# Attention's last head: layer-norm parts at every pair of source blocks, and the widest unit of targets second in a head

## The chip, the cores and the metric

The kernel runs on one core of a Trainium2 chip. The metric is the device time of one execution in microseconds (us). Five engines work side by side and are tied by semaphores: PE (TensorE, matmuls), ACT (ScalarE), DVE (VectorE), POOL (GpSimd) and SP (SyncE, which here issues the DMAs). An instruction waits in its engine's order until what it needs is done.

## The reference

A graph of 6250 nodes with 128 features and 206,250 directed edges (100,000 drawn both ways, and a loop at each node) goes through four graph layers. Each is followed by a residual and a layer norm:

```python
x = _layernorm(x + _L0_gnn_ref(...))   # mean of the neighbours, two products
x = _layernorm(x + _L1_gnn_ref(...))   # a two-layer product for every edge, mean over the edges of a target
x = _layernorm(x + _L2_gnn_ref(...))   # sums over the neighbours, two products
x = _layernorm(x + _L3_gnn_ref(...))   # attention, four heads of 32 features
```

The change lies in the last one, attention:

```python
h = (x @ W).reshape(N, H, C)                       # H = 4 heads, C = 32
logits = a_src[src] + a_dst[dst]
logits = jnp.where(logits > 0, logits, 0.2 * logits)
e = jnp.exp(logits - seg_max[dst])
alpha = e / (segment_sum(e, dst)[dst] + 1e-16)
out = segment_sum(h[src] * alpha[:, :, None], dst)
out = out.reshape(N, H * C) + bias
out = (out - mean) * rsqrt(var + 1e-05) * gamma + beta
return relu(out)
```

So a node's row passes two layer norms at the end: the one inside attention, then relu, the residual, and the outer one, whose result is the output.

## The kernel before, in words

The first three layers take the time up to about 3950 us and are not touched. Attention (`attend`, line 1107) works without gathers. The graph stands in HBM as a dense matrix of edge counts, `adj`, in bf16, cut into blocks of 128 source nodes by 256 targets. 6250 nodes make 49 source blocks. The targets make 12 groups of 512 and a last group of 106 (line 99). Two groups form a unit (line 1120), and the last, small group is joined to the sixth unit as its `more` (line 1122): five units of 1024 targets and a wide one of 1130. A pass of one unit in one head is called a step here: 4 heads x 6 units = 24 steps, in the order of `steps` (line 1247).

A step runs over the 49 source blocks in 25 pairs (line 1283; the last pair has one block). For each pair:
- SP loads the pair's block of `adj` into `A` three pairs ahead (`load`, line 1250; four buffers), and for the wide unit a narrow block into `Am`.
- ACT makes `r`, one instruction for each of the two blocks (line 1293), from the target's and the source's terms. It has two buffers.
- DVE takes the minimum `B` of `A` and `r` (line 1300) and the difference `C` of `A` and `B` (line 1302): the edges whose logits are on one side of zero, and the rest. In a wide step two more instructions do the same for the 106 targets (`Bm`, lines 1306 and 1307).
- PE multiplies the head's tables with `B`, `A` and `C` and adds up in PSUM over the step (line 1320, ten matmuls of 512 columns a pair; line 1322 for the 106 targets).

Everything else is let in between the pairs by hand, by three lanes (`Lane`, line 1226). A lane holds generators. `step(now)`, called once after each pair, runs the first generator up to its next `yield`, if `now` has reached `due`. Then `due` is set to now plus what was yielded, or plus 2 where nothing was; a generator that ends sets it to `now`, so that the next begins at the next pair. The lanes are:
- `sums`: `targets` (line 1180) prepares the target terms of the next step (transposes on PE, copies by ACT, lines 1186 and 1194). `close` (line 1197) finishes the step before: ACT and DVE copy the sums out of PSUM (lines 1202, 1205), PE folds them (line 1212), and four small DVE instructions divide (lines 1216 to 1221), for each group. In the last head it then hands `finish3` of the group to `ends` (line 1224).
- `news`: `tables` (line 1158) makes the next head's tables, group after group, four parts each: two DVE instructions (lines 1164, 1166), then three casts by ACT (line 1169), with a subtraction on POOL (line 1171) after the first two, and a DVE instruction with the next group's first part (line 1174). It is added at a head's second step (line 1282); what is left of it when the next head begins is run then (line 1280).
- `ends`: `finish3` (line 617) with `layernorm` (line 351) and `update` (line 369). Its parts, one for each `yield`: add and statistics (DVE); square root (ACT, line 361); reciprocal and scaling (DVE, lines 363, 365); gain and offset (DVE, lines 622, 623); relu (ACT, line 625); residual and statistics (DVE); square root (ACT); reciprocal and scaling (DVE); and then the store, issued by SP (line 126).

After the last step the lanes are emptied, one after the other (last line of `attend`): `close` of the last unit, then all of `ends`.

Of the kernel before, what the change touches and what calls it, by code (L numbers as in the profile page):

```python
# [68 lines left out]
def kernel(  # L69
# [688 lines left out]
    def fast():  # L758
# [348 lines left out]
        def attend(acc, al):  # L1107
# [12 lines left out]
            units = [(g[0][0], g, []) for g in (groups[k : k + 2] for k in range(0, len(groups), 2))]  # L1120
            if len(units) > 1 and len(units[-1][1]) == 1 and units[-1][1][0][2] == 1:
                units[-2][2].extend(units.pop()[1])
            with tc.tile_pool(name="f3c", bufs=1) as one, tc.tile_pool(name="f3", bufs=2) as ep, \
                    tc.tile_pool(name="f3n", bufs=1) as pool, \
                    tc.tile_pool(name="f3s", bufs=6, space=PSUM) as sps, \
# [100 lines left out]
                class Lane:  # L1226


                    def __init__(self):
                        self.left, self.due = [], 0  # L1230

                    def add(self, fn):
                        self.left.append(fn)
# [1 line left out]
                    def step(self, now):  # L1235
                        if self.left and now >= self.due:
                            lag = next(self.left[0], self)
                            if lag is self:
                                self.left.pop(0)
                            self.due = now if lag is self else now + (lag or 2)  # L1240

                    def rest(self):
                        while self.left:
# [16 lines left out]
                            nc.sync.dma_start(more_of[i][:, :n].rearrange("p l q -> p (l q)"),  # L1260
                                              adj[more[0][0] // (2 * P), :, a * 2 * P : (a + n) * 2 * P])

                sums, news, ends = Lane(), Lane(), Lane()
                for i in range(3):
                    load(i)
                drain(targets(0, *steps[0]))
# [1 line left out]
                made, i, now = 0, 0, 0  # L1268
# [69 lines left out]
        with tc.tile_pool(name="facc", bufs=1) as one:  # L1338
            acc = one.tile([P, 3, NA], F32, name="acc")
            for k in range(3):  # L1340
                nc.vector.memset(acc[:, k, :], 0.0)

            two, third = [acc[:, k, 0 : NB * D].bitcast(BF16).rearrange("p (b k d) -> p k b d", k=2, d=D) for k in (1, 2)]
            parts = [two[:, 0], two[:, 1], third[:, 0]]
            mlp("f1", lambda *a: node1(acc, parts, *a))
            al = one.tile([P, 2, NB, HEADS], F32, name="al")
            nc.vector.memset(al, 0.0)
            dense2(parts, lambda *a: node2(acc, al, *a))
            attend(acc, al)
# [39 lines left out]
```

## Time and profile before

| | us |
|---|---|
| median of 3 runs | 5586.52 (5569.49 to 5587.32) |
| profiled execution, its own time | 5547.28 |
| its span, first to last instruction | 5545.3 |
| first to last B of attention (line 1300) | 3958.39 to 5478.63 |
| PE busy over the span | 4983.3 (90%) |
| DVE busy | 3011.7 (54%) |
| ACT busy | 2590.3 (47%) |
| POOL busy | 1927.6 (35%) |
| mean granted TensorE clock | 0.94 |

The shares are means over stages with different limits, so they say little about attention alone. The steps of the last head, from the first B of each to the next step's first B, take 59.38, 62.69, 64.92, 64.47, 62.45 and, for the wide step, 74.12 to its last B; 66.67 are left from there to the span's end. In the third head they take 59.21, 60.70, 60.12, 60.22, 60.03 and 67.34. A row of a timeline has the start in us from the span's start, the length in us, engine, line, operation, out<-in with shapes, the count, and in brackets the idle time before it and what ended it.

### The profile page before, as it was taken

How to read it: one execution, taken by the hardware profiler on the slowest of the kernel's cores; microseconds unless marked ns; L12 is line 12 of the kernel's file. 1: busy time of each engine (PE TensorE's matmuls, PEld its weight loads, DVE VectorE, ACT ScalarE, POOL GpSimd, SP SyncE). 2: the span in 40 equal slices, each digit the busy share in tenths (PEclk: the TensorE clock that was granted, in tenths of full speed). 3: DMA queues.
4: the chain of work that ended last, by engine and by line, in shares of the span. 5: the costliest groups of instructions: out<-in, count | busy, mean ns of one | idle time of the engine just before them, and what ended most of it. 6: DMA issues, size and time to landing. Idle time of an engine off the chain costs nothing. (4 is left out here: it accounts for less than half of the span.)

```text
span 5545.3 us, 90483 instructions
## 1 busy us (share of the span) xinstructions
PE 4983.3 (90%) x33855; PEld 4094.6 (74%) x33855; DVE 3011.7 (54%) x5036; ACT 2590.3 (47%) x3581; POOL 1927.6 (35%) x1919
## 2 busy tenths in 40 slices
PE   1999997899999999998999999899799999999995
PEld 0899997888888888888888888699555655555553
DVE  4787874233333333333333333222488888888998
ACT  2444442332323333333322333100499999998884
POOL 2232223665666666666666665000111010010000
PEclk9999998898989988889988999899899999999997
DMA  3433323444444444444444443455367777777773
GB/s 75 130 143 120 142 114 128 128 129 123 128 123 129 129 127 127 124 124 129 130 123 127 126 125 102 163 187 187 120 200 218 224 213 227 217 210 227 212 211 119
DMA packets 587578, 837.61 MB, mean 151 GB/s; under 512 B 117853, under 2 KB 482330, under 8 KB 576384
## 3 DMA queue, kind: packets, MB, share of 16 engines
q1 hardware_dynamic: 502537, 605.23, 35.4%
q0 software_dynamic: 83472, 224.21, 14.0%
q8 instruction: 271, 4.44, 0.3%
q10 hardware_dynamic: 1124, 2.31, 0.1%
q14 instruction: 174, 1.43, 0.1%
HBM read 739.88 MB, written 91.53 MB: 150 GB/s over the span
## 5 line engine op out<-in xcount | busy, mean ns | idle before, releaser
L129 POOL DMA_INDIRECT g<-t,src_i x1617 | 1578.1, 976 | 965.0 <-issue 735.9
L1293 ACT ACTIVATE r<-ad,bias 128x1024 bf16<-128x1024 f32 (+1 forms) x1176 | 1276.7, 1155 | 91.1 <-DVE B L1300 55.4
L1068 DVE TENSOR_TENSOR g<-g,pre 128x512 f32<-128x512 f32 x882 | 549.5, 641 | 1340.5 <-PE pre L1066 406.8
L1320 PEld LDWEIGHTS <-acc 128*99 128x99 bf16 x5856 | 698.2, 126 | 606.5 <-issue 157.2
L1080 PE MATMUL seg<-oh,g 128*128 128x64 f32 (+1 forms) x6468 | 1026.1, 282 | 36.6 <-issue 34.5
L1066 PE MATMUL pre<-W1s,eaT 128*128 128x256 f32 (+1 forms) x3234 | 900.9, 420 | 117.9 <-DVE g L1068 68.2
L1080 PEld LDWEIGHTS seg<-oh,g 128*128 128x128 f32 (+1 forms) x6468 | 950.8, 203 | 75.0 <-issue 43.2
L1320 PE MATMUL s<-B,acc 128*99 128x512 bf16 x3504 | 885.1, 382 | 89.3 <-DVE B L1300 83.4
L1069 ACT ACTIVATE g<-g 128x512 f32<-128x512 f32 x882 | 506.7, 592 | 714.9 <-DVE g L1068 506.4
L1066 PEld LDWEIGHTS pre<-W1s,eaT 128*128 128x128 f32 (+1 forms) x3234 | 638.3, 210 | 250.5 <-issue 121.2
L1300 DVE TENSOR_TENSOR B<-A,r 128x2048 bf16<-128x2048 bf16 x600 | 724.5, 1207 | 118.8 <-ACT r L1293 91.4
L1057 ACT COPY eaT<-tp 128x512 f32<-128x512 f32 (+1 forms) x441 | 241.2, 547 | 1038.8 <-PE tp L1055 341.1
L1080 PE MATMUL seg<-oh,ea 128*128 128x64 f32 (+1 forms) x3234 | 659.6, 286 | 25.2 <-issue 24.9
L1080 PEld LDWEIGHTS seg<-oh,ea 128*128 128x128 f32 (+1 forms) x3234 | 523.0, 203 | 24.6 <-issue 24.3
L930 ACT CAST A<-pa 128x784 bf16<-128x784 f32 x400 | 322.8, 813 | 328.2 <-PE pa L927 319.6
L800 PE MATMUL sum<-A,xs 128*128 128x256 bf16 (+1 forms) x3675 | 467.1, 273 | 0.0
L1302 DVE TENSOR_TENSOR C<-A,B 128x1024 bf16<-128x1024 bf16 x600 | 429.6, 716 | 64.9 <-PE s L1320 2.4
L1171 POOL TENSOR_TENSOR xs<-xs,acc 128x264 f32<-128x264 f32 (+1 forms) x104 | 103.2, 999 | 985.4 <-ACT acc L1169 985.4
L800 PE MATMUL sum<-A,acc 128*128 128x256 bf16 (+1 forms) x3675 | 407.6, 271 | 8.6 <-DMA A<-adj 8.6
L927 PE MATMUL pa<-oh,oh 128*128 128x98 bf16 x3200 | 356.2, 269 | 59.6 <-ACT A L930 56.1
L800 PEld LDWEIGHTS <-acc 128*128 128x128 bf16 x3675 | 355.0, 98 | 49.2 <-issue 8.9
L800 PEld LDWEIGHTS <-xs 128*128 128x128 bf16 x3675 | 357.4, 101 | 34.6
(230 smaller groups left out, 4422.2 us busy)
## 6 DMA issues: line engine op xcount, KB each, us to landing
A<-adj SPq DMA_DIRECT2D x2304, 128.0 KB
ea<-in_edge_attr_dram SPq DMA_DIRECT2D x292, 256.0 KB
A<-adj SPq DMA_DIRECT2D x25, 1600.0 KB
A<-adj SPq DMA_DIRECT2D x25, 1536.0 KB
ea<-in_edge_attr_dram SPq DMA_DIRECT2D x146, 192.0 KB
g<-t,src_i POOLq DMA_INDIRECT x1617
Am<-adj SPq DMA_DIRECT2D x96, 128.0 KB
t<-y SPq DMA_DIRECT2D x24, 256.0 KB
```

What stands on the lines that cost most here:

```text
L129: nc.gpsimd.indirect_dma_start(out=to, out_offset=None, in_=table, in_offset=bass.IndirectOffsetOnAxis(ap=index[:K, t : t + 1], axis=0))
L800: nc.tensor.matmul(ps[:, :n], parts[part][:, b, :], a(b)[:, :n], start=k == 0, stop=k == 3 * NB - 1)
L927: nc.tensor.matmul(ps[:, o, q * LO : (q + 1) * LO], ohs[g][0][:, 2 * j + o, :, q], ohs[g][1][:, 2 * j + o, :, q], start=True, stop=True)
L930: nc.scalar.copy(A[sb][:, :, q0 : q0 + 2 * QI].rearrange("p k (o q) -> p k o q", q=QI), ps[:, :, : QI * LO].rearrange("p o (q k) -> p k o ...
L1066: nc.tensor.matmul(pre[:K, t, :], eaT[i][:, b + t, :K], W1s[:, 1, :], start=True, stop=True)
L1068: nc.vector.tensor_add(gb, gb, pre[:K, :n, :])
L1069: nc.scalar.activation(gb, gb, AF.Relu)
L1080: nc.tensor.matmul(ps[:, m, :], rows, oh[c][:K, a + t, :], start=a + t == 0 and m == 0, stop=a + t == T - 1, skip_group_check=True)
L1293: nc.scalar.activation(r[:, l, : n + m], ad[:, : n + m], AF.Relu, bias=bias[:, b + l, h : h + 1], scale=BIG)
L1300: nc.vector.tensor_tensor(wide(bt), At[:, :ns, :kk, :w], wide(r), ALU.min)
L1302: nc.vector.tensor_sub(ct[:, :n].rearrange("p (s q) -> p s q", q=w), At[:, :ns, 0, :w], bt[:, 0, :n].rearrange("p (s q) -> p s q", q=w))
L1320: nc.tensor.matmul(s[to][g][:M, : c1 - c0], row, rhs(c0, c1), start=to not in begun, stop=stop)
```

## The change

Two edits in `attend`. The wide unit, when the small group has been joined to it, is taken out of the last place of the list of units and put at the second. The list is used by all four heads. And a lane gets its lag as an argument: `ends` is made with 1, so that a part of `finish3` follows after one pair and not two; `sums` and `news` keep 2. Line numbers behind line 1122 grow by one.

```diff
             if len(units) > 1 and len(units[-1][1]) == 1 and units[-1][1][0][2] == 1:
                 units[-2][2].extend(units.pop()[1])
+                units.insert(1, units.pop())
...
-                    def __init__(self):
-                        self.left, self.due = [], 0
+                    def __init__(self, lag=2):
+                        self.left, self.due, self.lag = [], 0, lag
...
-                            self.due = now if lag is self else now + (lag or 2)
+                            self.due = now if lag is self else now + (lag or self.lag)
...
-                sums, news, ends = Lane(), Lane(), Lane()
+                sums, news, ends = Lane(), Lane(), Lane(1)
```

## The prediction

> **What bounds the kernel now.** I read the page first, for the stages. A digit is the busy share of one of 40 slices of 138.6 us; attention fills slices 29 to 40.
>
> ```profile
> PE   1999997899999999998999999899799999999995
> DVE  4787874233333333333333333222488888888998
> ACT  2444442332323333333322333100499999998884
> DMA  3433323444444444444444443455367777777773
> ```
>
> In attention PE and ACT show 9 and DVE 8, and in the last two full slices the order turns: DVE 9, ACT 8. A row so coarse cannot say who sets the pace. So I cut attention into its steps, a step being one unit of targets in one head, 25 pairs of source blocks, from its first B (line 1300) to the next step's. Columns: the stretch, its length, then busy us of PE, PEld, DVE, ACT and POOL. Overlapping instructions are counted once.
>
> ```profile
> 4842.89:4903.01 60.12, 57.99 (x285) 35.03 (x284) 52.38 (x72) 56.23 (x64) 6.26 (x7) 1.00 0.72 214
> 5023.26:5090.60 67.34, 65.46 (x407) 41.04 (x406) 60.58 (x111) 59.44 (x56) 1.21 (x1) 1.00 0.82 241
> 5090.60:5149.98 59.38, 57.47 (x288) 35.14 (x287) 51.21 (x66) 53.98 (x55) 0.00 (x0) 1.00 0.71 213
> 5277.59:5342.06 64.47, 59.63 (x290) 35.62 (x289) 61.17 (x113) 56.91 (x59) 0.00 (x0) 1.00 0.71 212
> 5404.51:5478.63 74.12, 64.92 (x385) 39.79 (x384) 68.65 (x150) 57.45 (x53) 0.00 (x0) 0.98 0.70 209
> 5478.63:5545.30 66.67, 7.76 (x54) 6.20 (x52) 47.23 (x181) 8.24 (x21) 0.00 (x0) 0.56 0.07 22
> ```
>
> Row 1 is an ordinary step of the third head: PE fills it, DVE has 8 us to spare. Row 2 is its wide step: DVE and PE are both near the limit. Row 3, the fourth head's first step, has no layer norms and takes 59.38. Rows 4 and 5 have them: DVE is now the fullest engine and the steps are longer, 64.47 and 74.12. Row 6 is the tail: PE has stopped and layer norms run alone. So the work that the change pulls out of the tail goes to an engine that is already the bound. The rows of DVE inside row 4 give the prices (start, length):
>
> ```profile
> 5322.08 1.23 DVE L1300 TENSOR_TENSOR B<-A,r 128x2048 bf16<-128x2048 bf16 x1
> 5323.41 0.69 DVE L1302 TENSOR_TENSOR C<-A,B 128x1024 bf16<-128x1024 bf16 x1
> 5324.02 0.68 DVE L373 TENSOR_TENSOR res<-o,xn 128x512 f32<-128x512 f32 x1
> 5324.74 0.87 DVE L356 BATCH_NORM_STATS2 st<-res 128x6 f32<-128x128 f32 x4
> 5325.53 0.36 DVE L358 BATCH_NORM_AGGREGATE mv<-st 128x2 f32<-128x6 f32 x4
> 5325.92 1.23 DVE L1300 TENSOR_TENSOR B<-A,r 128x2048 bf16<-128x2048 bf16 x1
> ```
>
> A pair costs DVE 1.93 us from B to B; this one, with one part of a layer norm, 3.84. DVE never pauses. ACT in the same stretch:
>
> ```profile
> 5317.27 0.62 ACT L625 ACTIVATE o<-o 128x512 f32<-128x512 f32 x1
> 5317.79 8.42 ACT L1293 ACTIVATE r<-ad,bias 128x1024 bf16<-128x1024 f32 x8
> 5326.11 0.29 ACT L361 ACTIVATE rs<-mv,eps 128x4 f32<-128x4 f32 x1
> ```
>
> Two r of 1.04 make a pair, so ACT needs 2.08 and runs up to two pairs ahead (r has two buffers). The square root of the part above stands two pairs later, and when ACT reaches it the statistics are nearly or quite there.
>
> **The change, part by part.** *The tail shrinks.* A group's layer norms (lines 617 to 628; I count them as one job) are eight parts and a store. At a part every second pair a job holds its lane for 17 pairs, and a step's two for 34 of 25: the lane falls behind. At a part a pair they hold it for 18, and it keeps up. Followed through the steps, before leaves five full jobs and the small one (106 rows) for the tail; after leaves two full ones.
>
> ```profile
> 5488.64 0.68 DVE L620 TENSOR_TENSOR o<-acc,gbc 128x512 f32<-128x512 f32 x1
> ...
> 5497.83 0.68 DVE L620 TENSOR_TENSOR o<-acc,gbc 128x512 f32<-128x512 f32 x1
> ```
>
> The five take 5488.64 to 5534.86, 9.24 each; the small one 4.6. Gone: 3 x 9.24 + 4.6 = 32.3. The close loses its third group (1.0, 5487.63 to 5488.64) and the last pair its narrow products (about 0.6). The last store is a full one instead of a small one; a full store's packets end 2.0 us after its last operation, so I add nothing. Tail: -33.9.
>
> *Jobs in the loop.* Ten full ones and the small one, where seven were. A full one costs DVE 1.91 (add, statistics), 1.24 (reciprocal, scale), 1.33 (gain, offset), 1.91, 1.24: 7.63, read from pairs of 3.84, 3.17 and 3.26 against 1.93. In wide pairs (2.51) the differences are smaller, together 7.0. The small one's rows sum to 3.1.
>
> *A new wait.* With one pair between parts, the square root stands on ACT behind the r of the very next pair, and waits there for statistics that DVE finishes only as it starts that pair's B. Behind it in ACT's queue is the r two pairs on, whose buffer was free long before. From that B: 0.03 to release, 0.30 square root, 2.08 for r, 0.04 to DVE: the B after next can start at 2.45 and not 1.93. DVE loses 0.5, and PE, fed by DVE, too. The relu (0.52 net) loses 0.8 likewise. A full job has two roots and a relu: 1.8. In the wide step, where DVE takes 2.51 a pair, 0.9. Before has no such wait, so I bound it: zero, if ACT gets r out ahead after all (less is excluded: a wait gives nothing back), and 2.3, three times the mean wait of r for B between 5277.59 and 5404.5 (12.3 us in 16). I take 1.8, since each term is a row.
>
> *The fourth head, summed.* A step without jobs holds DVE for 24 x 1.93 + 1.4, the close's copies 1.2 and two times 1.28: 51.5. Two jobs, their waits, and 0.9 for the close's ACT copies (line 1202, seen in pairs of 2.65 to 2.70 where DVE had no backlog): 51.5 + 15.3 + 3.6 + 0.9 = 71.3, four times. The wide step: 67.3 + 14.0 + 1.8 = 83.1. The third group's close and the small job, now inside: 1.0 + 3.1 + 1.5 of waits = 5.6. With the first step: 59.4 + 83.1 + 285.2 + 5.6 - 1.4 (last pair, counted to its B) = 431.9, against 388.0 measured (5090.60 to 5478.63): +43.9. The same sum made for before gives 383, 5 short. Fourth head with tail: 43.9 - 33.9 = +10.0.
>
> *The first three heads.* The lane of tables (line 1158) starts at a head's second step and takes a part every second pair, so before it is over three pairs into the wide step. After, the wide step is the second and carries 12.5 parts, 3.1 groups. In ordinary steps these hide under PE's pace; in the wide step DVE has no room. One group costs DVE 0.54 (pair of 2.47) and, through its two GpSimd subtractions, C of 0.97 for 0.69 and pairs of 2.22 and 2.39: 0.29 + 0.46. Together 1.29, x 3.1 = 4.0. The Trainium skill (SBUF — State Buffer, Who interferes with whom) speaks against the change harder: a VectorE instruction with two SBUF inputs and a GpSimd one that reads SBUF take an exclusive lock, and the second is blocked until the first ends. A GpSimd subtraction averages 1.14 here, so by the rule a group costs up to 0.54 + 2.28 = 2.8 and a wide step 8.7. The rows show 0.28 to 0.46 of each subtraction reaching DVE; I use them. The last step of a head now lacks tables: 59.3 for 60.1, -0.8. The three-group close moves from the first step to the third: PE work moved, zero net, 0.9 either way. ACT's wide step (59.4, plus 3.8 of casts) and the loads, issued by SP in the same numbers, stay below 71. Per head +3.2; three heads +9.6. The unit order alone has no other price: SP's stores stand one pair behind the last part, before a load that waits for a later event.
>
> **Sum.** +10.0 + 9.6 = +19.6. The profiled execution takes 5547.28 (span 5545.3), and would take 5566.9; it lies 39 under the median of the runs, 5586.52, and nothing in the change bears on that gap, so 5606.
>
> **The rivals.** Differences within 0.3% (16.7 us) can't be told from none.
> - *ACT is not held.* Then all 21.3 of waits go and the change ends at -1.7: 5585, not slower. For it: r has two buffers, and ACT waited just 0.4 at a root before. Against: the root stands ahead of the next r in one queue. It decides where less than a tenth of the waits is left.
> - *The tables cost nothing in the wide step.* +10: 5596, within 0.3%. For: 1.7 us of pairs there are stretched by other waits. Against: DVE's pairs of 2.51 have no gap.
> - *The lock at full price.* Three wide steps at 8.7 for 4.0, +14 more: 5620. For: the rule. Against: the rows of C.
> - *The loop swallows the parts*, as if PE set the pace: -34: 5553. Against: rows 4 and 5.
>
> **Chances.** Forecast 0.55 (about 12 to 28 slower, 0.42 of it beyond 0.3%), ACT not held 0.14, free tables 0.13, dearer 0.13, swallowed 0.05. Slower 0.42 + 0.13 = 0.55; same 0.13 + 0.14 + 0.13 = 0.40; faster 0.05. The range runs from below the second rival's and the first's time, with their runs' spread, to above the dear case: 5578 to 5626.
>
> **What would show it.** A tail of about 33 us after the last B; four steps of the fourth head near 71 and its wide step near 83; r on ACT idle behind a root or relu, with pairs of 2.4 and 2.7 where no DVE part stands; wide steps of the first three heads at 71 and last ones at 59. If the fourth head's steps stay near 67, the wait is wrong; if near 62, DVE is not the bound.

## The result and the profile after

The changed kernel takes 5595.99 us (median of 14 runs, 5578.76 to 5616.84), the kernel before 5585.56 (14 runs beside it). The ratio is 1.0018 with a 95% interval of 1.0005 to 1.0031: slower by 0.18%, some 10 us. That is inside the range of the prediction and has its sign, but less than the 19.6 us forecast.

The profiled execution has a span of 5592.2, 46.9 more than before's 5545.3. Most of that is not the change: the first B of attention starts at 3996.4 and not at 3958.4, behind three layers that are the same instruction for instruction. From the first B to the span's end it is 1595.8 against 1586.9, +9.0, which fits the paired runs. All sums below are made from there.

First the page's busy digits for the stages (to be read at the right end: DVE stays at 8 and 9 there, ACT and the loads fall):

```profile
PE   1999997899899998998998999899799999999886
DVE  4788774232333333333333333222488888888988
ACT  2444442332333323333332323100489999899775
DMA  3433333444444444444444443455377777777664
```

Then attention by steps, as before (length, then busy us of PE, PEld, DVE, ACT and POOL): the third head's third and wide step, its last step, and in the fourth head the first, the wide, an ordinary and the last step to its last B, and the tail.

```profile
4889.49:4950.18 60.69, 58.43 (x290) 35.40 (x288) 53.78 (x76) 56.61 (x65) 6.22 (x7) 1.00 0.71 211
4819.83:4889.49 69.66, 66.32 (x410) 41.28 (x409) 64.30 (x121) 61.87 (x63) 7.06 (x6) 1.00 0.79 235
5070.11:5129.00 58.89, 57.49 (x285) 34.90 (x284) 50.18 (x61) 54.04 (x56) 1.20 (x1) 1.00 0.74 218
5129.00:5187.69 58.69, 57.76 (x287) 35.26 (x286) 50.44 (x61) 53.60 (x55) 0.00 (x0) 1.00 0.74 222
5187.69:5269.41 81.72, 69.67 (x409) 42.39 (x408) 74.56 (x171) 61.73 (x61) 0.00 (x0) 0.98 0.69 207
5416.92:5487.78 70.86, 58.57 (x281) 34.54 (x281) 64.16 (x121) 54.43 (x59) 0.00 (x0) 1.00 0.65 190
5558.20:5592.20 34.00, 7.33 (x44) 5.71 (x42) 20.20 (x73) 3.52 (x8) 0.00 (x0) 0.60 0.06 18
```

The tail has gone from 66.67 to 34.00. The ordinary step of the fourth head has gone from 64.47 and 62.45 to 70.86, the wide one from 74.12 (to its last B) to 81.72. And there is more in it than DVE's work: DVE is busy 64.16 of 70.86, where before it was busy 61.17 of 64.47. Something makes DVE wait. Summed:

| us | before | after | difference |
|---|---|---|---|
| first three heads | 1132.2 | 1132.6 | +0.4 |
| fourth head, first to last B | 388.0 | 429.2 | +41.2 |
| tail | 66.6 | 34.0 | -32.6 |

What DVE waits for shows in its timeline, one job (one group's layer norms) in an ordinary step:

```profile
5463.17 1.22 DVE L1301 TENSOR_TENSOR B<-A,r 128x2048 bf16<-128x2048 bf16 x1
5464.49 0.69 DVE L1303 TENSOR_TENSOR C<-A,B 128x1024 bf16<-128x1024 bf16 x1
5465.58 1.23 DVE L1301 TENSOR_TENSOR B<-A,r 128x2048 bf16<-128x2048 bf16 x1 [0.39 <-DMA A<-adj]
...
5472.02 1.22 DVE L1301 TENSOR_TENSOR B<-A,r 128x2048 bf16<-128x2048 bf16 x1
5473.34 0.69 DVE L1303 TENSOR_TENSOR C<-A,B 128x1024 bf16<-128x1024 bf16 x1
5474.88 1.23 DVE L1301 TENSOR_TENSOR B<-A,r 128x2048 bf16<-128x2048 bf16 x1 [0.84 <-DMA A<-adj]
```

and ACT's in the same stretch:

```profile
5463.17 0.30 ACT L361 ACTIVATE rs<-mv,eps 128x4 f32<-128x4 f32 x1 [2.27 <-DVE mv L358]
5463.37 6.33 ACT L1294 ACTIVATE r<-ad,bias 128x1024 bf16<-128x1024 f32 x6
5472.14 0.63 ACT L625 ACTIVATE o<-o 128x512 f32<-128x512 f32 x1 [2.43 <-DVE o L623]
5472.67 4.25 ACT L1294 ACTIVATE r<-ad,bias 128x1024 bf16<-128x1024 f32 x4
```

From B to B it is 2.41 and 2.86 in place of 1.93: the forecast said 2.45 and 2.7. ACT stands idle at the root for 2.27 us and at the relu for 2.43, and only then starts the two r for the next pair, from 5463.37 and 5472.67. The second of each two, by itself:

```profile
5464.41 1.13 ACT L1294 ACTIVATE r<-ad,bias 128x1024 bf16<-128x1024 f32 x1
5473.71 1.13 ACT L1294 ACTIVATE r<-ad,bias 128x1024 bf16<-128x1024 f32 x1
```

They end at 5465.54 and 5474.84, and both times B starts 0.04 us later. The brackets of B name the load of A, not r. B waits for both, and the profile puts a wait down to the release it saw last. The label alone would send one to the DMA; the rows of ACT, and the runs below in which the loads are the same and the waits are gone, say r.

### The profile page after: what moved, and what is told of

The parts are those of the page before. It is cut to its first block, busy times and chain, and to the rows that moved or that the text cites. A ratio compares the mean times of both kernels' runs of the same rounds, so it can differ in the third digit from the quotient of the medians.

```text
span 5592.2 us, 90479 instructions
## 1 busy us (share of the span) xinstructions
PE 5002.8 (89%) x33855; PEld 4104.1 (73%) x33855; DVE 3013.2 (54%) x5036; ACT 2584.6 (46%) x3581; POOL 1922.6 (34%) x1919
## 4 chain that ended last, share of the span: by engine, by line
PE 42%; DVE 5%; ACT 5%; issue 3%; DMA 2%; another core or an unknown queue 1%; POOL 1%; SPq 1%; DVEq 0%; POOLq 0%; ACTq 0%
PE s L1321 13%; PE seg L1080 9%; PE sum L800 7%; PE pre L1066 7%; ACT r L1294 4%; DVE B L1301 2%; DMA A<-adj 2%; PE tp L1055 2%; PE na L1213 1%; SPq L1257 1%; PE na L450 1%; DVE sT L1206 0%; DVE C L1303 0%; PE sm L1323 0%
## 5 line engine op out<-in xcount | busy, mean ns | idle before, releaser
L1080 PE MATMUL seg<-oh,g 128*128 128x64 f32 (+1 forms) x6468 | 1038.1, 284 | 45.0 <-issue 41.9
L1080 PEld LDWEIGHTS seg<-oh,g 128*128 128x128 f32 (+1 forms) x6468 | 962.7, 205 | 84.8 <-issue 53.6
```

Source lines behind the costliest of these rows:

```text
L1080: nc.tensor.matmul(ps[:, m, :], rows, oh[c][:K, a + t, :], start=a + t == 0 and m == 0, stop=a + t == T - 1, skip_group_check=True)
```

## The experiments

Three theories stood against each other. Mine: the loop pays for DVE's work of each job that moves, and on top for ACT's queue being held at roots and relu that come too early. Against it: ACT holds nothing and DVE's work is all. The other: the order of the units makes the loss. For each run, the fourth head from first to last B, the tail, and their sum, from its profile (before: 388.0 + 66.6 = 454.7; after: 429.2 + 34.0 = 463.2):

| run | loop | tail | sum | ratio to before (95%) |
|---|---|---|---|---|
| order alone | 384.1 | 70.3 | 454.4 | 1.0002 (0.9993 to 1.0010) |
| lag alone | 426.9 | 39.8 | 466.8 | 1.0023 (1.0014 to 1.0031) |
| gap where ACT reads | 404.1 | 43.3 | 447.4 | 0.9985 (0.9978 to 0.9993) |
| relu on DVE | 421.0 | 32.3 | 453.3 | 1.0002 (0.9993 to 1.0010) |
| relu and gap | 408.4 | 32.2 | 440.6 | 0.9982 (0.9964 to 1.0000) |
| the same again | 407.8 | 32.5 | 440.3 | 0.9980 (0.9963 to 0.9996) |
| relu and gap, wide unit last | 405.4 | 37.8 | 443.2 | 0.9988 (0.9972 to 1.0004) |
| before, with relu on DVE | 391.0 | 54.0 | 445.1 | 0.9990 (0.9973 to 1.0007) |
| gain and offset on GpSimd | 415.6 | 37.9 | 453.5 | 0.9995 (0.9976 to 1.0014) |
| all jobs in the tail | 358.6 | 132.5 | 491.1 | 1.0059 (1.0037 to 1.0081) |

The first four ran on one chip, where the kernel before takes 5089 us; the others on chips where it takes 5545 to 5548. The three layers ahead of attention make that difference (the first B comes near 3500 or near 3960); attention's steps agree to tenths.

**The two edits apart.** The order with the lane's old lag:

```diff
-                sums, news, ends = Lane(), Lane(), Lane(1)
+                sums, news, ends = Lane(), Lane(), Lane()
```

> The new order of the units alone; the layer norms' lane keeps a part every second pair. My theory: the roots and the relu stand two pairs behind and hold nothing, so the fourth head's pairs are 1.93 plus their DVE parts, none of 2.41 or 2.86. Seven jobs, one of them the small one, are done in the loop and six full ones are left for the tail: tail about 70 us after the last B (66.7 before), loop of the fourth head about 385 (388 before), together within 3 us of before. The first three heads as in the changed kernel: wide step 69.5, last step 58.8, sums unchanged. Ratio to before 1.000. Rival (the order costs what the change loses): 1.0018 and ordinary steps of the fourth head near 71.

Measured: 384.1 + 70.3, and the steps of the first three heads like those of the changed kernel. The order alone changes nothing that can be measured. The lag alone, with the wide unit last:

```diff
-                units.insert(1, units.pop())
```

> A part at every pair alone; the wide unit stays last in a head. My theory: all of the loss comes from here. Ten full jobs in the loop, each with two pairs of 2.41 behind its roots and one of 2.86 behind its relu: four steps of the fourth head near 71 and the wide step, now the last, near 80 to its last B; the tail keeps two full jobs and the small one and takes about 39. Together about 7 us over before, ratio 1.0012; the first three heads step by step as before (60.1 and 67.4). Rival (the order makes the loss, the lag is free): ratio 0.995, steps near 66.

Measured +12.1 by the trace and +0.23%, more than I had expected: the ordinary steps take 71.9 to 72.5, not 71. The pairs are as expected (2.41, 2.86). So the lag makes the loss, and the order, with it, takes 3.6 of it back (466.8 to 463.2) by the traces, one of each kernel; the intervals of the two ratios overlap.

**Is it the wait?** The lag is kept, and only behind a DVE part that ACT reads next, two pairs are left:

```diff
-    def layernorm(pool, t, to, rows, nb):
+    def layernorm(pool, t, to, rows, nb, gap=None):
...
             nc.vector.bn_aggr(mv[:rows, b, :], st[:rows, b, :])
-        yield
+        yield gap
...
         nc.vector.tensor_add(o[:rows, :nb], o[:rows, :nb], gb[2])
-        yield
+        yield gap
...
-        ends.add(finish3(..., pool, m0, rows, nb))
+        ends.add(finish3(..., pool, m0, rows, nb, 2 if nb > 1 else None))
```

> The changed kernel, but in the full jobs two pairs lie between a DVE part and the ACT part that reads it (root, relu), and one pair everywhere else. The DVE work of a job is the same. My theory (ACT's queue holds r): the pairs of 2.41 and 2.86 vanish, 1.9 us a full job; ordinary steps of the fourth head fall from 71 to 67 and the wide one from 81.7 to 80. Eight full jobs and part of a ninth fit into the loop, which leaves the tail about 7 us longer (41) and the loop shorter by that job's parts. Sum 12 us below the changed kernel, 4 below before: ratio 0.999. Rival (DVE's own work is all of the cost, the waits only move): ratio as changed, 1.002, with steps still near 71.

The work is the same and the loads are the same. The ordinary steps fall to 67.1 to 68.4 (the last one, to its last B, from 70.4 to 65.4), and ACT in this run finds its operands there (no bracket at root and relu):

```profile
4954.75 2.19 ACT L1294 ACTIVATE r<-ad,bias 128x1024 bf16<-128x1024 f32 x2 [0.69 <-DVE B L1301]
4956.87 0.63 ACT L625 ACTIVATE o<-o 128x512 f32<-128x512 f32 x1
4958.01 6.34 ACT L1294 ACTIVATE r<-ad,bias 128x1024 bf16<-128x1024 f32 x6 [0.51 <-DVE B L1301]
4964.46 0.30 ACT L361 ACTIVATE rs<-mv,eps 128x4 f32<-128x4 f32 x1
```

The step that took 70.86 in the changed kernel, with as many DVE instructions (121) and DVE busy 63.44 where it was 64.16, takes 67.08:

```profile
4905.81:4972.89 67.08, 58.13 (x283) 34.89 (x282) 63.44 (x121) 55.92 (x59) 0.00 (x0) 1.00 0.66 200
```

The sum falls by 15.8, and this kernel is faster than before by 0.15%. That is more than the 12 expected: the pairs beside the close's ACT copies, 3.18 and 3.04 us in two steps of the changed kernel, are down to 1.94 as well. That DVE's work is all of the cost is out: with the work unchanged, the waits alone decide the sign. The same from another side, taking the relu off ACT:

```diff
-        nc.vector.tensor_add(t[:rows, :nb], po[:rows, :nb], (xb if plus is None else plus)[:rows, :nb])
+        if relu:
+            nc.vector.scalar_tensor_tensor(t[:rows, :nb], po[:rows, :nb], 0.0, xb[:rows, :nb], op0=ALU.max, op1=ALU.add)
...
-        nc.scalar.activation(o[:rows, :nb], o[:rows, :nb], AF.Relu)
-        yield
-        xb = yield from update(pool, o, n0, rows, nb)
+        xb = yield from update(pool, o, n0, rows, nb, relu=True)
```

> The changed kernel with the relu taken off ACT: the residual's DVE instruction (line 373) becomes max with zero, then add, so a job has one ACT part less and no relu part. My theory: pairs of 2.86 vanish and those of 2.41 stay: 0.93 less in each of eight full jobs, 0.5 in the wide ones and the small one, 9 us in the loop; the tail loses 0.7 a job, 1.4. Ordinary steps near 69. Sum 10 us under the changed kernel, 2 under before: ratio 1.000. Rival (the relu's wait is not the cause): steps near 71 and only the tail's 1.4 gained, ratio 1.0016. A DVE instruction of this kind that is slower than the add's 0.69 would show in pairs of more than 3.84.

Measured: 9.9 less than the changed kernel. In the ordinary steps the pairs of 2.86 are gone and those of 2.41 are still there; the steps themselves take 70.1 to 72.4, above the 69 expected. The new instruction costs what the add cost (0.69 us). Both together, so that a full job has no ACT part queued too early (the gap now only where `layernorm` yields after its statistics):

```diff
+        xb = yield from update(pool, o, n0, rows, nb, relu=True, gap=gap)
```

> The relu in the residual's DVE instruction, and two pairs between statistics and root in the full jobs; one pair elsewhere. No ACT part is left that is queued too early. My theory: pairs of 2.41 and 2.86 are all gone; eight full jobs fit into the loop and two are left, 0.7 shorter each: fourth head's loop about 413, tail 33, together 446, 9 under before and 17 under the changed kernel; ratio to before 0.998. Ordinary steps near 67. Rival (the longer job falls behind its lane and brings the tail back): tail near 42, ratio 0.999 or more.

Measured: 440.6, 22.6 under the changed kernel and 14.1 under before by the trace. The loop fell further than I had said (408 against 413), and no ordinary step has a pair of 2.41 or 2.86 left.

**What does DVE's work cost in the loop?** The kernel before, with the lane left standing in the loop:

```diff
-                        for lane in (sums, news, ends):
+                        for lane in (sums, news):
```

> The kernel before with the layer norms' lane left standing until the loop is over: all thirteen jobs in the tail. My theory: up to a point the jobs fill DVE's slack under PE's pace, beyond it each costs its full 7.6. The loop of the fourth head without jobs takes 361 (steps of 59.1, wide 67.3), so before's seven jobs cost 27 in the loop, 3.9 each, where the next three cost 7.6 and with the waits 9.5. Tail 131. Together 38 over before, ratio 1.007. Rival (a job costs 7.6 in the loop from the first): loop 335, ratio 1.002.

Measured: a loop without jobs takes 358.6. Before's seven jobs thus add 29.5 to it, 4.2 each, less than DVE's 7.6 for one, since DVE has slack until it passes PE. In the kernel with relu and gap, three more and the small one add 20.4 (408.4 - 388.0), nearer to the full price: the three jobs' 22.9 and the small one's 3.1 would be 26. So of the 41.2 us that the change adds to the loop, about 20.4 are the work that came in. The other 20.8 (429.2 - 408.4) go when the early roots and relus go, and the seven jobs that stood in the loop before pay their part of them too. A job in the loop is cheaper than the 9.24 (8.5 with the relu fused) that it takes in the tail as long as it brings no wait; at its full 7.6 and with 1.9 of waits it is not. The window of an ordinary step without jobs:

```profile
5277.33:5335.86 58.53, 57.39 (x284) 34.91 (x283) 50.26 (x60) 53.20 (x54) 0.00 (x0) 1.00 0.73 220
```

PE is busy 57.39 of 58.53, DVE 50.26. That gap of 8 us is the room that the first job of a step fills.

Then gain and offset were taken off DVE, in the version with relu and gap:

```diff
-        nc.vector.tensor_mul(o[:rows, :nb], o[:rows, :nb], gb[1])
-        nc.vector.tensor_add(o[:rows, :nb], o[:rows, :nb], gb[2])
-        yield
+        nc.gpsimd.tensor_mul(o[:rows, :nb], o[:rows, :nb], gb[1])
+        nc.gpsimd.tensor_add(o[:rows, :nb], o[:rows, :nb], gb[2])
+        yield gap
```

> As the run before, with gain and offset (lines 622, 623) on GpSimd, which has nothing else to do in the fourth head; two pairs behind them too. My theory (DVE's time is what the loop pays): 1.33 of DVE less a job, about 0.7 of it given back where GpSimd slows DVE, as it did at the tables (0.28 to 0.46 for each instruction): 5 us less in the loop, about 2 more in the tail, where GpSimd's instructions are slower than DVE's 0.69; together 443. By the skill's rule (SBUF — State Buffer, Who interferes with whom: the second of the two is blocked for the whole instruction) two GpSimd instructions of about 1.1 each would cost DVE up to 2.2 for the 1.33 saved: 455, no better than before.

A miss: 453.5, 12.9 more than without, 7.2 of it in the loop and 5.7 in the tail. DVE in this kernel, while GpSimd runs the two (5364.15 for 2.12 us, 5366.35 for 1.60):

```profile
5365.24 1.57 DVE L1304 TENSOR_TENSOR C<-A,B 128x1024 bf16<-128x1024 bf16 x1
5366.74 2.29 DVE L1302 TENSOR_TENSOR B<-A,r 128x2048 bf16<-128x2048 bf16 x1
```

C takes 1.57 for 0.69, B 2.29 for 1.22: 1.95 lost for 1.33 saved, and much the same in other jobs of ordinary steps. In the tail, with DVE waiting for them, the two take 1.26 each; a job there takes 9.8 and not 8.5, and DVE waits 2.6 us longer for PE's folds in the last close, for which no run gives the reason. Here the Trainium skill's rule of the exclusive lock (SBUF — State Buffer, Who interferes with whom) was the better guide, an estimate of 2.2 by my reading of it, than the price carried over from the tables (0.7).

**The first three heads.** The changed kernel with tables made in the first head only; the third and fourth head multiply with stale tables:

```diff
-                        news.add(tables(h + 1, groups))
+                        if h == 0:
+                            news.add(tables(h + 1, groups))
```

> The changed kernel without the tables of the third and the fourth head: their lane runs in the first head only, and heads three and four use stale tables. It prices the tables in the second and third head, whose lane is then empty. My theory: they cost 1.1 to 1.6 in an ordinary step, through ACT's casts and DVE's waits, and 2.3 in the wide one; without them ordinary steps take 59.1 and the wide step 67.3, and heads two and three 362 instead of 368. Then the change moved 3.1 groups from an ordinary step (where they cost 1.3, not nothing) to the wide one (2.3), and the price of that move is 1 a head and not 3.2. Rival (the tables are free in ordinary steps, as I took it): ordinary steps stay at 60.1 to 60.7 without tables.

The second head's third step (ordinary) and wide step of this kernel, with no tables to make:

```profile
4477.72:4536.93 59.21, 57.30 (x288) 35.06 (x287) 51.25 (x66) 53.89 (x55) 0.00 (x0) 1.00 0.71 213
4409.95:4477.72 67.77, 66.07 (x410) 41.35 (x409) 60.54 (x110) 59.22 (x54) 0.00 (x0) 1.00 0.80 242
```

With tables the third head takes 60.69 and 69.66 there, as shown above. So 3.1 groups cost about 1.4 in an ordinary step (0.9 to 1.7) and about 2.1 in the wide one (67.2 to 67.8 without, 69.5 to 69.7 with). Both whole heads take 360.8 without tables and 368.4 with, and before's took 368.3: the tables cost 7.6 a head, and it made no difference which steps they stood in. The traces of the other runs say the same: the first three heads take 1131.5 to 1133.8 with the wide unit last and 1132.0 to 1133.6 with it second. What the move costs is below that spread of 2 us.

Where the wide step found room for tables shows in two places of it, in the second head. Without tables, in this run:

```profile
4412.73 1.23 DVE L1302 TENSOR_TENSOR B<-A,r 128x2048 bf16<-128x2048 bf16 x1 [0.33 <-ACT sT L1203]
4416.02 1.22 DVE L1302 TENSOR_TENSOR B<-A,r 128x2048 bf16<-128x2048 bf16 x1 [0.84 <-DMA A<-adj]
...
4441.93 1.23 DVE L1302 TENSOR_TENSOR B<-A,r 128x2048 bf16<-128x2048 bf16 x1
4445.37 1.22 DVE L1302 TENSOR_TENSOR B<-A,r 128x2048 bf16<-128x2048 bf16 x1 [0.98 <-DMA Am<-adj]
```

and the same two pairs with tables, in the changed kernel:

```profile
4454.00 1.22 DVE L1301 TENSOR_TENSOR B<-A,r 128x2048 bf16<-128x2048 bf16 x1
4456.51 1.23 DVE L1301 TENSOR_TENSOR B<-A,r 128x2048 bf16<-128x2048 bf16 x1
...
4483.91 1.23 DVE L1301 TENSOR_TENSOR B<-A,r 128x2048 bf16<-128x2048 bf16 x1
4486.63 1.23 DVE L1301 TENSOR_TENSOR B<-A,r 128x2048 bf16<-128x2048 bf16 x1 [0.27 <-DMA Am<-adj]
```

The pairs of 3.29 and 3.44, beside ACT's copies for the close and the targets, are 2.51 and 2.72 when tables put work on DVE just before them. DVE is busy 3.7 us longer in this step with tables (64.27 against 60.54), and the step takes only 1.8 longer.

**What each part is worth once the waits are gone.** Three kernels on one chip. The first is the best version again, unchanged. The second is the same with the wide unit last (first diff, against the best). The third is the kernel before with the relu's edit and nothing else (second diff, against the changed kernel with the relu on DVE):

```diff
-                units.insert(1, units.pop())
```

```diff
-                units.insert(1, units.pop())
...
-                sums, news, ends = Lane(), Lane(), Lane(1)
+                sums, news, ends = Lane(), Lane(), Lane()
```

> The best version so far once more, beside two that lack a part of it: relu in the residual's DVE instruction, two pairs between statistics and root, wide unit second. Fourth head's loop 408 and tail 32 as measured (440.6; before 454.7), the first three heads as before: 12 us under before, ratio 0.998.

> The same with the wide unit last in a head, as before the change. My theory: the tail keeps the small job and the third group's close, 5.5 us, and loses as much or a little less in the loop; the two kernels without these waits then differ by 0 to 4 us, as the changed kernel and the one with the lag alone did (463.2 and 466.8). Fourth head and tail 441 to 445, ratio 0.998 to 0.9985. Rival (the order brings what it was measured to bring in the tail): 6 more than with the wide unit second.

> The kernel before with nothing but the relu in the residual's DVE instruction: lag 2, wide unit last. A job is seven parts and 15 pairs instead of 17, so eight full jobs fit into the loop and four and the small one are left, each 0.7 shorter. Loop 388 + 7 = 395, tail 66.6 - 9.2 - 3.3 = 54: together 449, 6 under before, ratio 0.999. If the lag and the order of the change matter at all once the waits are gone, this stays 8 us over the best version; if not, it equals it.

Sums 440.3, 443.2 and 445.1 (440.6, 441 to 445 and 449 expected). The intervals of the three overlap, so only the traces rank them, one of each kernel: of the 14.4 us between before and the best, fusing the relu brings 9.6 by itself (6 expected), and lag, gap and order 4.8 more (8 expected). The best version is faster than before by 0.20% (interval 0.04 to 0.37%). It and the kernel with the gap alone (0.15%) beat both the kernel before and the changed one.

## Why the prediction was right, and where it was not

In sum: the fourth head with its tail came out at +8.6 (+10.0 forecast), the first three heads at +0.4 (+9.6). The measured +10 lies just under the 12 to 28 of the forecast and, at 0.18%, inside the 0.3% within which the prediction calls two kernels the same, to which it gave 0.40 against 0.55 for slower.

- *The tail* (-33.9): measured -32.6. The jobs left are the two that were counted, 9.2 each. The saving in the close was overestimated: from the last B to the first job it takes 9.36 against 10.01, 0.65 less and not 1.6, since DVE waits 0.7 us longer for PE's folds between the two groups (1.96 against 1.26).
- *The new wait* (1.8 a job): right in mechanism and size. Pairs behind a root 0.48 longer, behind a relu 0.93; 1.9 a job in ordinary steps, 1.4 for the two jobs of the wide step together, where pairs of 2.51 become 2.59 and 3.04 (1.8 forecast). The run that removed it returned 15.8, of 12 expected; the run that removed the relu's part 9.9, of 10.
- *The fourth head's sum* (431.9): measured 429.2. Ordinary steps 70.9 and, to its last B, 70.4 (71.3 and 69.9), the wide one 81.7 (83.1), the two with the small job in them 73.1 and 74.4, together 5.8 over two ordinary ones (5.6).
- *The first three heads* (+9.6): measured +0.4. This is the step that failed, the sentence that tables in ordinary steps "hide under PE's pace; in the wide step DVE has no room". They do not hide: they cost 0.9 to 1.7 there too, as the run without tables shows, and a last step without them is 1.1 to 1.8 under the ordinary ones of before in the second and third head, not 0.8. And the wide step had room. DVE's added time there is 3.7, near the 4.0 counted, and single pairs are longer by 0.27 to 0.69; but pairs that had stood waiting, 3.29 and 3.44 us long without tables, became shorter by 1.5 together. So the wide step is 69.5 to 69.7 and not 71: about 2.0 of the 4.0 was paid. The prediction's trace had such pairs (3.35 and 3.43 in the second head's wide step). The rival of the free tables named them, and I gave it 0.13.
- *The rivals.* Of "ACT is not held" nothing is left. "The tables cost nothing in the wide step" is what happened in sum, by another balance: about +2.0 there, and as much back in the other steps. Its 5596 against a median of 5595.99 is luck to the tenth. The lock at full price was not met at the tables, but nearly was in the run with GpSimd (1.95 of the estimated 2.2).

## What to carry to other kernels

When work is fed by hand between the pairs of a loop, count for each part not only what it costs its own engine but how far behind its producer it is queued: on an engine that works in order and runs ahead, a consumer placed one iteration early holds everything behind it. Here the distance, not the amount of work, decided between slower and faster. Work moved from a tail into a loop is cheap until the slack of the engine that does it is gone, and a second small instruction fused into a neighbour (max and add in one) can be worth more than the scheduling, as it was here by the traces (9.6 against 4.8 us).

## What was not expected of the hardware

A scalar_tensor_tensor with max and add on 128x512 f32 took 0.69 us on DVE, as long as the plain add. GpSimd's elementwise instruction of that size took 1.26 alone (spans on this engine are rough) and 2.12 and 1.60 beside DVE's bf16 ones, which grew from 0.69 to 1.57 and from 1.22 to 2.29 at the same time: both sides lose.
